# A Mamba scan on one Trainium2 core: last states through dA's first token, more C products on GpSimd, a later gate and a fourth C buffer

## The chip, the cores and the metric

The kernel runs on one core of one Trainium2 chip. The metric is the device time of one execution in microseconds (us). The core has five engines with a queue of instructions each: TensorE (PE in the profile), VectorE (DVE), ScalarE (ACT), GpSimd (POOL) and SyncE (SP), which issues nearly all DMAs here. An engine takes its instructions in order; one that waits holds back all behind it.

## What is computed

The reference runs two "metaformer" layers on x of shape (2, 96, 128, 128). Nearly all time goes to the mixer of layer 0, four Mamba scans (rows forward and backward, columns forward and backward) of 16,384 tokens, each with 192 channels and 16 states:

```python
def step(h, t):
    dt_t, u_t, B_t, C_t = t
    dA = jnp.exp(dt_t[:, :, None] * A)
    h = dA * h + dt_t[:, :, None] * B_t[:, None, :] * u_t[:, :, None]
    y = jnp.einsum('bds,bs->bd', h, C_t)
    return (h, y)
...
xz = x @ in_w.T                      # split into xc and z
xc = silu(conv4(xc) + conv_b)        # along the tokens
dt_raw, Bm, Cm = split(xc @ xproj_w.T)
dt = softplus(dt_raw @ dt_w.T + dt_b);  A = -exp(A_log)
y = (scan + Dp * xc) * silu(z);  out = y @ outp_w.T
```

The four results are joined, projected and added to x. Behind it come a quantized feed-forward layer, a 3x3 convolution and another feed-forward layer.

## The kernel before

For each of the two images the kernel normalizes x (`normalize`), runs the scans (`mamba`) and then the rest (`ffn_and_conv`). The change is in `mamba`.

**Tiles.** Two scans run together, a row scan and a column scan, so 2 x 192 channels fill three groups g of 128 partitions. The tokens go in blocks of T = 512. A *step* is one block of one pair: 32 blocks x 2 pairs = 64 steps an image, 128 in all. Within a step a *unit* is a group and two states; 3 x 8 = 24 units, numbered 0 to 23 (group 0 has 0 to 7, and so on). Unit k of the next step is written k'.

**The work of a unit.** ScalarE makes dA = exp(dt * A) for two states into a PSUM tile `da` (L349, three buffers, made two units ahead). A DMA broadcasts four states' B rows to 128 partitions (tile `row0`, 1 MB, for two units; L335), and GpSimd multiplies it by dt * u (`b_part`, L339). VectorE scans each state along the 512 tokens (`scan`, L353). The states are multiplied by the C rows (tile `row1`, again 1 MB for two units), on VectorE (L441) or, for units listed in `BY_POOL`, on GpSimd (`by_pool`, L360); for those the scan writes into the B tile instead of `da`. TensorE adds the products over the states with identity matmuls into the PSUM tile `y` (`sums`, L357; one buffer). After a group's eight units VectorE multiplies `y` by silu(z) (`gated`, the *gate*, L364), and TensorE starts the next group's `y` with the skip term (L448).

**State from step to step.** ScalarE copies each unit's last states to `hst` (L442). At the next step it makes `enter` = exp(dt of the first token * A) for a group (`entry`, L303); GpSimd multiplies that by `hst` (L342) and adds it to the first token of each B product (L343). The scan starts from 0.

**The order** is written out by hand in one loop over units; I call a turn of it *slot* k, and D(k) the time at which its first scan starts:

```python
if k % 2 == 0:
    fetch(k + 2 * B_AHEAD, 0, B_AHEAD, bs)   # B tile of units k+6, k+7
    feed(k + AHEAD)                          # GpSimd: B product of k+2, k+3
issue(k, 0)                                  # planned pieces
scan(0, da, b, hs[k])
behind(k - 1)     # C product, copy to hst, gate at a group's begin, sums
feed_decay(k + AHEAD)                        # ScalarE: dA of unit k+2
scan(1, da, b, hs[k])
if k % 2 == 0:
    fetch(k + 2 * C_AHEAD, 1, C_AHEAD, cs)   # C tile
issue(k, 1)                                  # planned pieces
```

`fetch` has as many buffers as it is ahead plus one, so each DMA, B or C, goes into the buffer that units k-2 and k-1 used. All stand in SyncE's one queue. F(k) is GpSimd's B product for units k and k+1, P(k) its C product of unit k, S(k) the sums of unit k; B(k) and C(k) are the DMAs of the tiles of units k and k+1. For a unit on GpSimd, P(k) is put in GpSimd's queue at the end of slot k+1, and S(k) in TensorE's at the end of slot k+3; for the others S(k) comes in slot k+1.

**Planned pieces** prepare the step after (`prologue`): at slot 21 the DMAs of its input, xa and xb (L228); at slots 1, 5 and 9 the input projection with the convolution folded in (*inx*, L211) of groups 1, 0, 2; at 7, 18 and 21 that of the z half (*inz*, L211, copied out at L247); silu of xc at slot 11 and of z at slot 7 (L259), softplus of dt at the end of slot 17 (L293), each between two table loads; the B, C and dt rows at slot 12; dt at 14 to 17 (L284, L289); dt * u (*dtu*, L298) at 19, and at 3 and 5 of the next step. At slots 19 and 3 of a step its outputs go through *project* (L372, L374) and are copied out. inx, inz, rows, dt and project share one PSUM tile, `misc`.

## Time and profile before

| | |
|---|---|
| median of 3 runs | 11,550.82 us (11,549.54 to 11,551.47) |
| the profiled execution, its own time | 11,556.77 us |
| its span | 11,555.0 us |
| PE, DVE, ACT, POOL busy over the span | 90%, 90%, 68%, 84% |
| one step in the middle of the second pair | 79.09 us |
| DMA | 3,417 MB, 87% of the 16 engines' time within a step |

The profile is one execution; times in it are us, or ns where marked. A line such as L357 is a line of the kernel. In a timeline the columns are start, length, engine, line, operation, output<-inputs, count, and in brackets the idle time ahead with what ended it. A matmul of 512 columns in f32 leaves two records, so a unit's sums are four. In a list of waits, the columns are the total, the number and the longest.

### The profile page before, as it was taken

To read this page: it belongs to the slowest core of one execution; us is meant where nothing else is said; L and a number is where in the kernel's file an instruction comes from. 1 tells how busy PE (TensorE), PEld (TensorE's weight loads), DVE (VectorE), ACT (ScalarE), POOL (GpSimd) and SP (SyncE) were. 2 spreads that over 40 slices of the span, in tenths; PEclk is the share of its full clock that TensorE was granted. 3 is DMA by queue.
4 is the path that set the end of the run, shared out by engine and by line. 5 is a ranking of instruction groups with operands and counts; after the bars stand their busy time and mean duration, and the time that the engine had idled before them with its cause. 6 is when DMAs were issued, how large, how long until landed. Compare 5 with 4: busy or idle time off the path is not lost. (4 is left out here: it accounts for less than half of the span.)

```text
span 11555.0 us, 94102 instructions
## 1 busy us (share of the span) xinstructions
PE 10435.0 (90%) x24208; PEld 3971.4 (34%) x24208; DVE 10421.6 (90%) x10127; ACT 7901.7 (68%) x13564; POOL 9672.3 (84%) x4700
## 2 busy tenths in 40 slices
PE   7999999999999999989989999999999999999899
PEld 2333333333333333333323333333333333333333
DVE  6999999999999999994469999999999999999944
ACT  6767767677677677665567677677676776776655
POOL 5999999999999999991159999999999999999911
PEclk8999999999999999999989999999999999999999
DMA  7888888888888888880068888888888888888800
GB/s 263 335 329 333 333 332 332 330 331 333 329 332 333 330 331 333 329 322 19 26 243 334 328 331 334 330 333 333 333 331 329 332 332 329 331 333 329 319 13 13
DMA packets 540755, 3416.96 MB, mean 296 GB/s; under 512 B 67532, under 2 KB 68652, under 8 KB 143832
## 3 DMA queue, kind: packets, MB, share of 16 engines
q1 hardware_dynamic: 539960, 3410.16, 76.8%
q8 instruction: 196, 3.21, 0.1%
q14 instruction: 343, 2.81, 0.1%
q0 software_dynamic: 256, 0.79, 0.0%
HBM read 3289.04 MB, written 54.53 MB: 289 GB/s over the span
## 5 line engine op out<-in xcount | busy, mean ns | idle before, releaser
L339 POOL TENSOR_TENSOR row<-dtu,row 128x2048 f32<-128x2048 f32 x1536 | 6948.9, 4524 | 283.3 <-DMA row<-bcd 281.6
L357 PE MATMUL y<-row,ident 128*128 128x512 f32 x12288 | 5690.6, 603 | 700.0 <-DVE row L441 699.9
L353 DVE TENSOR_TENSOR_SCAN da<-da,row 128x512 f32<-128x512 f32 x4608 | 5456.9, 1214 | 38.9 <-ACT da L349 5.2
L349 ACT ACTIVATE da<-dt,amat 128x512 f32<-128x512 f32 x6144 | 4246.9, 691 | 170.2
L357 PEld LDWEIGHTS y<-row,ident 128*128 128x128 f32 x12288 | 2256.8, 190 | 4008.4 <-issue 2243.5
L441 DVE TENSOR_TENSOR row<-da,row 128x1024 f32<-128x1024 f32 x2304 | 2776.7, 1205 | 70.2 <-DMA row<-bcd 70.0
L442 ACT COPY hst<-da 128x2 f32<-128x2 f32 x2304 | 368.9, 160 | 2652.2 <-DVE row L441 2649.3
L360 POOL TENSOR_TENSOR row<-row,row 128x1024 f32<-128x1024 f32 x768 | 1807.4, 2353 | 223.0 <-DVE row L353 147.5
L353 DVE TENSOR_TENSOR_SCAN row<-da,row 128x512 f32<-128x512 f32 x1536 | 1852.4, 1206 | 91.9 <-POOL row L339 84.1
L211 PE MATMUL misc<-xa,inx 96*64 96x512 f32 (+1 forms) x2048 | 946.1, 605 | 50.0 <-ACT mix L239 26.8
L211 PE MATMUL misc<-xb,inx 96*64 96x512 f32 (+1 forms) x2048 | 952.3, 608 | 33.6 <-ACT hst L442 24.2
L564 POOL TENSOR_TENSOR acc<-acc,y 96x512 f32<-96x512 f32 x128 | 147.4, 1151 | 991.5 <-DVE y L563 991.5
L298 POOL TENSOR_TENSOR dtu<-dt,xc 128x512 f32<-128x512 f32 x384 | 487.4, 1269 | 106.0 <-DMA xb<-xnc 99.8
L576 PE MATMUL pc<-pad,kw 96*96 96x512 f32 x1152 | 566.4, 593 | 0.0
L211 PEld LDWEIGHTS misc<-xa,inx 96*64 96x64 f32 (+1 forms) x2048 | 327.3, 165 | 581.2 <-issue 438.0
L448 PE MATMUL y<-xc,dmat 128*128 128x512 f32 x768 | 419.5, 628 | 103.6 <-DVE sz L364 103.6
L374 PE MATMUL misc<-sz,gmat 128*96 128x512 f32 x1024 | 484.1, 595 | 0.0
L284 PE MATMUL misc<-rows,dtw 12*128 12x512 f32 x768 | 434.3, 645 | 50.6 <-ACT dt L289 37.9
L364 DVE TENSOR_TENSOR sz<-y,sz 128x512 f32<-128x512 f32 x384 | 264.6, 689 | 229.5 <-PE y L357 198.0
L136 DVE TENSOR_TENSOR xq<-xm,rs 96x512 fp8e5<-96x512 f32 x128 | 87.9, 687 | 392.2 <-ACT rs L132 392.2
L211 PEld LDWEIGHTS misc<-xb,inx 96*64 96x64 f32 (+1 forms) x2048 | 316.5, 164 | 361.9 <-issue 214.1
L372 PE MATMUL misc<-acc,ident 96*96 96x512 f32 x512 | 387.6, 842 | 57.3 <-ACT sz L247 53.8
(76 smaller groups left out, 7449.9 us busy)
## 6 DMA issues: line engine op xcount, KB each, us to landing
row<-bcd SPq DMA_DIRECT2D x3072, 1024.0 KB, 7.4
xc<-mix SPq DMA_DIRECT2D x256, 128.0 KB, 5.4
sz<-mix SPq DMA_DIRECT2D x256, 128.0 KB, 8.9
xa<-xnr SPq DMA_DIRECT2D x124, 193.1 KB, 8.6
xb<-xnc SPq DMA_DIRECT2D x124, 193.1 KB, 8.7
bcd<-rows SPq DMA_DIRECT2D x128, 128.0 KB, 9.5
acc<-in_x_dram SPq DMA_DIRECT2D x16, 768.0 KB, 5.7
xnr<-xn SPq DMA_DIRECT2D x16, 768.0 KB, 4.3
```

Source lines behind the costliest of these rows:

```text
L211: nc.tensor.matmul(ps[rows, :], w(PAIRS[pi][d], k, lo, hi), src[d][:, k : k + T], **se)
L284: nc.tensor.matmul(d["ps"], w, d["rows"][0 : 2 * RK, :], start=True, stop=True)
L298: nc.gpsimd.tensor_tensor(dtu, d["dt"][:, g, :], d["xc"][:, g, :], ALU.mult)
L339: nc.gpsimd.tensor_tensor(b, d["dtu"][g][:, None, :].broadcast_to((128, 4, T)), b, ALU.mult)
L349: nc.scalar.activation(da[:, j, :], d["dt"][:, g, :], AF.Exp, scale=amat[:, pi, g, s + j : s + j + 1])
L353: nc.vector.tensor_tensor_scan(h[:, j, :], da[:, j, :], b[:, j, :], 0.0, ALU.mult, ALU.add)
L357: nc.tensor.matmul(y, ident, c[:, j, :], start=False, stop=s + j == S - 1)
L360: nc.gpsimd.tensor_tensor(c, h, c, ALU.mult)
L374: nc.tensor.matmul(d["po"], gmat[:, pi, 2 * g - 2 + k, :], d["yg"][g - 1 + k], start=False, stop=k == 1)
L441: nc.vector.tensor_tensor(c, h, c, ALU.mult)
L448: nc.tensor.matmul(y, dmat[:, pi, g, :], d["xc"][:, g, :], start=True, stop=False)
L576: nc.tensor.matmul(pc, kw[:, t, :], rows, start=t == 0, stop=t == 8)
```

## The change

The last states no longer enter through B. After the two exponentials of a unit, ScalarE multiplies the first token of each dA by the last state of that row of channels (a product on one column, in PSUM, with a pointer operand), and the scan starts from 1 instead of 0: the first step of the recursion then gives dA * h + B. `enter`, `entry` and GpSimd's products and adds on it are gone.

`BY_POOL` was units 0, 4, 8, 12, 16, 20; it is now 0, 3, 5, 8, 11, 13, 16, 19. As their sums come late, the last matmul of a group's `y` is that of unit 5, 13 and 23 (`LAST`). For a group's first unit `behind` now comes after the second scan of the slot, and with it the gate. The C tiles are fetched three pairs of units ahead, with four buffers, instead of two with three. The scratch for dynamic DMAs is set to 4,096.

```diff
-C_AHEAD = 2
+C_AHEAD = 3
-BY_POOL = tuple((g, s) for g in range(3) for s in (0, 8))
+BY_POOL = ((0, 0), (0, 6), (0, 10), (1, 0), (1, 6), (1, 10), (2, 0), (2, 6))
+LAST = [max(range(0, S, 2), key=lambda s: s + 5 * ((g, s) in BY_POOL)) for g in range(NG)]
...
-                def entry(g):
-                    nc.scalar.activation(enter[:, g, :], amat[:, pi, g, :], AF.Exp, scale=d["dt"][:, g, 0:1])
...
-            def b_part(i, d, g, s, b):
+            def b_part(d, g, b):
                 nc.gpsimd.tensor_tensor(b, d["dtu"][g][:, None, :].broadcast_to((128, 4, T)), b, ALU.mult)
-                if i > 0:
-                    if s == 0:
-                        nc.gpsimd.tensor_tensor(enter[:, g, :], enter[:, g, :], hst[:, g, :], ALU.mult)
-                    nc.gpsimd.tensor_tensor(b[:, :, 0], b[:, :, 0], enter[:, g, s : s + 4], ALU.add)
...
+                if i > 0:
+                    for j in range(2):
+                        nc.scalar.activation(da[:, j, 0:1], da[:, j, 0:1], AF.Copy, scale=hst[:, g, s + j : s + j + 1])
                 return da
...
-                nc.vector.tensor_tensor_scan(h[:, j, :], da[:, j, :], b[:, j, :], 0.0, ALU.mult, ALU.add)
+                nc.vector.tensor_tensor_scan(h[:, j, :], da[:, j, :], b[:, j, :], float(i > 0), ALU.mult, ALU.add)
...
-                    nc.tensor.matmul(y, ident, c[:, j, :], start=False, stop=s + j == S - 1)
+                    nc.tensor.matmul(y, ident, c[:, j, :], start=False, stop=(s, j) == (LAST[g], 1))
...
+            def gate_before(k):
+                pn, pu = divmod(k - 1, nu)
+                gated(steps[pn][0], state[pn], units[pu][0], ys.pop(k - 1))
+
+            def begins(k):
+                return 0 <= k < total and units[k % nu][1] == 0 and units[k % nu] in BY_POOL
...
-                if 0 < k <= total:
+                if 0 < k <= total and not begins(k - 1):
                     behind(k - 1)
                 feed_decay(k + AHEAD)
                 if k < total:
-                    scan(1, da, b, hs[k])
+                    scan(steps[n][1], 1, da, b, hs[k])
+                if begins(k - 1):
+                    behind(k - 1)
...
-    nc = bacc.Bacc("TRN2", target_bir_lowering=False, num_devices=1)
+    nc = bacc.Bacc("TRN2", target_bir_lowering=False, num_devices=1, dynamic_dma_scratch_size=4096)
```

More of the change, by code (lines that the diff above doesn't have):

```diff
@@ L194, in mamba @@
             hst = one.tile([128, NG, S], F32, name="hst")
-            enter = one.tile([128, NG, S], F32, name="enter")
             acc_w = acc.rearrange("c (h w) -> c w h", w=W)
@@ L321, in prologue @@
                     at += [(k, 0, partial(dt_u, g))]
-                    if i > 0:
-                        at += [((20, 24, 29)[g], 1, partial(entry, g))]
                 outs = (conv_out, gate_out, rows_out, dt_out)
@@ L336, in row_tile, with decay @@
                 return t
-            def b_part(i, d, g, s, b):
+            def b_part(d, g, b):
                 nc.gpsimd.tensor_tensor(b, d["dtu"][g][:, None, :].broadcast_to((128, 4, T)), b, ALU.mult)
-                if i > 0:
-                    if s == 0:
-                        nc.gpsimd.tensor_tensor(enter[:, g, :], enter[:, g, :], hst[:, g, :], ALU.mult)
-                    nc.gpsimd.tensor_tensor(b[:, :, 0], b[:, :, 0], enter[:, g, s : s + 4], ALU.add)
-            def decay(pi, d, g, s):
+            def decay(pi, i, d, g, s):
                 da = ps_w.tile([128, 2, T], F32, name="da")
@@ L349, in decay, with scan, sums @@
                     nc.scalar.activation(da[:, j, :], d["dt"][:, g, :], AF.Exp, scale=amat[:, pi, g, s + j : s + j + 1])
-                return da
-            def scan(j, da, b, h):
-                nc.vector.tensor_tensor_scan(h[:, j, :], da[:, j, :], b[:, j, :], 0.0, ALU.mult, ALU.add)
-            def sums(s, y, c):
+                if i > 0:
+                    for j in range(2):
+                        nc.scalar.activation(da[:, j, 0:1], da[:, j, 0:1], AF.Copy, scale=hst[:, g, s + j : s + j + 1])
+                return da
+            def scan(i, j, da, b, h):
+                nc.vector.tensor_tensor_scan(h[:, j, :], da[:, j, :], b[:, j, :], float(i > 0), ALU.mult, ALU.add)
+            def sums(g, s, y, c):
                 for j in range(2):
-                    nc.tensor.matmul(y, ident, c[:, j, :], start=False, stop=s + j == S - 1)
+                    nc.tensor.matmul(y, ident, c[:, j, :], start=False, stop=(s, j) == (LAST[g], 1))
             def by_pool(h, c):
@@ L425, in feed @@
                     n = k // nu
-                    b_part(steps[n][1], state[n], *units[k % nu], quads.pop(k))
+                    b_part(state[n], units[k % nu][0], quads.pop(k))
             def feed_decay(k):
@@ L430, in feed_decay @@
                     n = k // nu
-                    das[k] = decay(steps[n][0], state[n], *units[k % nu])
+                    das[k] = decay(*steps[n], state[n], *units[k % nu])
             ys = {}
+            def gate_before(k):
[3 more added lines that the diff above has]
+                return 0 <= k < total and units[k % nu][1] == 0 and units[k % nu] in BY_POOL
             def behind(k):
@@ L444, in behind @@
                     if k > 0:
-                        pn, pu = divmod(k - 1, nu)
-                        gated(steps[pn][0], state[pn], units[pu][0], ys.pop(k - 1))
+                        gate_before(k)
                     y = ps_y.tile([128, T], F32, name="y")
@@ L453, in behind @@
                     later(k + 1, 1, True, by_pool, h, c)
-                    later(k + 3, 1, True, sums, s, y, c)
+                    later(k + 3, 1, True, sums, g, s, y, c)
                 else:
-                    sums(s, y, c)
+                    sums(g, s, y, c)
                 if k == total - 1:
@@ L481, in mamba @@
                     hs[k] = b if (g, s) in BY_POOL else da
-                    scan(0, da, b, hs[k])
-                if 0 < k <= total:
+                    scan(steps[n][1], 0, da, b, hs[k])
+                if 0 < k <= total and not begins(k - 1):
                     behind(k - 1)
```

## The prediction

> **What bounds the kernel now.** I read the page's slices first (two stretches in which DVE, POOL and PE all show 9), then busy time over one step, then the waits of each engine, then the timelines of one step, engine by engine. Names are those of the section on the kernel: D(k) is when slot k begins, F, P and S are the B product, GpSimd's C product and the sums. The stage under change fills 128 steps of 79.09 us, 10,124 of 11,555 us. One step:

> ```profile
> core 0: us, PE busy (x) PEld busy (x) DVE busy (x) ACT busy (x) POOL busy (x), PEclk, DMA share, GB/s
> 8600.39:8679.48 79.09, 72.08 (x167) 28.16 (x167) 76.64 (x70) 55.85 (x97) 74.45 (x37) 1.00 0.87 332
> ```

> Four resources lie within 13% of each other, so no share of busy time prices this change; the order of the queues does. The waits (total us, times, longest):

> ```profile
> DVE sz L364 <- PE y L357: 198.0, 207, 3.1
> ...
> DVE row L441 <- DMA row<-bcd: 70.0, 121, 1.3
> ...
> POOL row L339 <- DMA row<-bcd: 281.6, 307, 3.6
> ...
> SPq L335 <- PE y L357: 6879.4, 1404, 11.1
> ```

> VectorE stalls little. But the DMA queue stands for 6,879 us behind C tiles whose buffer TensorE has not yet summed, and every later transfer stands behind them. ScalarE (first three lines) against VectorE (last two), around unit 13:

> ```profile
> 8641.74 1.28 ACT L260 ACT_TABLE_LOAD   x1
> 8643.03 0.16 ACT L442 COPY hst<-da 128x2 f32<-128x2 f32 x1
> 8643.23 1.42 ACT L349 ACTIVATE da<-dt,amat 128x512 f32<-128x512 f32 x2
> ```
> ```profile
> 8643.32 1.21 DVE L353 TENSOR_TENSOR_SCAN row<-da,row 128x512 f32<-128x512 f32 x1
> 8644.68 2.50 DVE L353 TENSOR_TENSOR_SCAN da<-da,row 128x512 f32<-128x512 f32 x2
> ```

> The scan starts 0.03 after the pair of exponentials ends (8643.23 + 1.42 = 8644.65), the same in the four steps behind it. After a silu (4.09 us with its two table loads) ScalarE is only just in time. At the end of the step, TensorE, then SyncE, then GpSimd:

> ```profile
> 8666.05 1.10 PE L372 MATMUL misc<-acc,ident 96*96 96x512 f32 x2 [0.42 <-ACT sz L247]
> 8666.99 1.88 PE L374 MATMUL misc<-sz,gmat 128*96 128x512 f32 x4
> 8668.71 5.31 PE L357 MATMUL y<-row,ident 128*128 128x512 f32 x12
> ```
> ```profile
> 8672.33 2.04 SPq L335 DMA_DIRECT2D row<-bcd  x3
> 8674.41 0.44 SPq L228 DMA_DIRECT2D xa<-xnr  x1
> 8674.89 0.44 SPq L228 DMA_DIRECT2D xb<-xnc  x1
> 8675.49 0.34 SPq L335 DMA_DIRECT2D row<-bcd  x1
> ```
> ```profile
> 8679.47 4.52 POOL L339 TENSOR_TENSOR row<-dtu,row 128x2048 f32<-128x2048 f32 x1 [0.62 <-DMA row<-bcd]
> 8684.07 0.20 POOL L343 TENSOR_TENSOR row<-row,enter 128x4 f32<-128x4 f32 x1
> 8684.23 2.36 POOL L360 TENSOR_TENSOR row<-row,row 128x1024 f32<-128x1024 f32 x1
> ```

> The twelve records are S(18), S(16), S(19). C(22) goes out as S(16) ends (8672.3), then B(2'), C(0') at 8674.05 as S(19) ends, xa, xb, B(4'). The four row tiles land 4.6, 6.7, 7.9 and 10.7 us after issue: 4.6 from a queue near empty, some 2.5 for each further one, 1.7 for xa and xb. F(2') starts when its tile lands; F(4') comes after P(0'), at 8686.55. Slot 0' begins at 8680.46, so B(4') goes out 5.0 us before it.

> **The change, by parts.** Pitches (start to start) from these timelines: scan and VectorE C product 1.12, gate 0.60, F 4.49, P 2.31, dtu 1.24, S 1.75 a unit, inx of group 1 3.6, of groups 0 and 2 3.44, project 3.49.

> *VectorE* loses two C products: 2.24 of 79.09 us. A slot is 3.36, or 2.24 where GpSimd has the product, 2.84 with a gate; 16, 5 and 3 of these make 73.5.

> *GpSimd* loses 12 adds (pitch 0.27 with the gap ahead, F to F 4.76) and 3 entry products (0.3), and gains two P: 12 x 4.49 + 8 x 2.31 + 3 x 1.24 = 76.1, against 12 x 4.76 + 6 x 2.31 + 3.7 + 0.9 = 75.6. No gain. Nor does VectorE hold GpSimd up: the six P of one step took 2.347 to 2.366, though scans and C products ran beside them.

> *ScalarE* loses three entry exponentials (0.29, hidden) and gains 48 products on one column. No row has it. Nearest: the copy of two columns out of PSUM, 0.160; a pointer operand adds 0.087 (L289 0.668 against L247 0.581); the upper end is the entry exponential, 0.294. I take 0.22 each, a little under 0.160 + 0.087 since it writes PSUM, and 0.04 of gap as between dependent instructions (L131 to L132): 0.52 a unit; 0.40 and 0.67 at the ends (0.160 and 0.294). Nothing less, since it only adds instructions. It is hidden in a plain slot, where ScalarE idles 1.1 to 1.8, but not behind a silu. [...]

> *Gate*: one scan later. Group 0's and 1's now wait for one more S (unit 5 or 13). It stood 1.55 us a step; I leave 0.5 to 0.8, inside the stretches below.

> *Fourth C buffer*: C goes out for two units further ahead, from the same slot and into the buffer of the same two units; the 0.55 us a step of L441 goes. It does not free the queue. Before, GpSimd's units are even: C of slot k waits for S(k-2), in TensorE's order one slot later. Now five of eight are odd: it waits for S(k-1), two slots later, after another unit's sums. Queued behind it on SyncE: the next B tile, at the step's end xa and xb too. That is the cost of this change. Odd units also free a B buffer later: before, P of a unit stood ahead of the next F in GpSimd's queue, now behind it; for unit 19 only F(0') lies between its P and F(2'), 4.49 against 5.2 from issue to start, which costs GpSimd 0.7 where it has slack. Smaller scratch: q0 carries 0.0%; nothing. The scan's initial 1.0: nothing.

> **Sum of a step.**
> Slots 10 to 13, ScalarE: before 10.33 (8634.35 to 8644.68), bound by pair, silu, pair; now two pairs are 0.52 longer, 11.35 (VectorE alone would need 8.96).
> Slots 13 to 16: 3.36 + 2.24 + 3.36 = 8.96.
> Slots 16 to 21: C product of unit 15 ends 2.33 after D(16); copy 0.23; pair 1.94; dt 0.6; pair 1.97; copy 0.1; softplus 4.09; copy 0.2; pair 1.94: D(20) at +13.5. Then sz 0.58, copy and pair: D(21) at +16.1. Before 17.5.
> Slots 21 to 24: three of 3.36, 10.1.
> Slots 0' to 10': project waits for that sz, D(16) + 14.0 (before + 12.2), which is 12.2 before D(0'). TensorE then runs through: project 3.49, S(18), S(16) 3.5, inz 0.97, S(20), S(21), S(19) 5.25: S(19) ends at D(0') + 1.05. C(2') waits for it, so it goes out at +1.1, then xa, xb, B(4') at +2.6; before, B(4') was out at -5.0. By the rows above C(2') lands at +5.7 and B(4') 4.2 later (10.7 - 7.9 + 1.4), +9.9. F(4') starts at +10.0 (before +6.1). From there GpSimd has no gap: F(4'), dtu, F(6'), P(3'), dtu, F(8'), P(5'), F(10') are 4 x 4.49 + 2 x 2.31 + 2 x 1.24 = 25.1. F(10') ends at +35.1, and slot 10' needs it. VectorE alone would be there at 30.3; it waits on the way, some 1.3 for F(4'), 2.5 for F(8'), 0.5 for F(10'). The other path is close: inx of group 1 needs xb (+7.4), and from there TensorE has 26.5 us without a gap up to the gate of slot 9' (inx 3.6, skip term 0.96, S of units 1, 2, 0, 4, 3, 6, 7, 5 at 14.0, project 3.49, inx of group 0 3.44, inz 1.0): gate at +33.9, D(10') at 34.5.
> Step: 35.1 + 11.35 + 8.96 + 16.1 + 10.1 = 81.6, that is 2.5 over 79.09. Some 126 steps see it (the ends of a batch do not): +315. The profiled execution took 11,556.8, 6 over the median, so 11,550.8 + 315 = 11,866.
> Bounds: six pairs lie in these stretches, so products at 0.40 to 0.67 move a step by -0.7 to +0.9; B(4') landing 1 us earlier moves it by -1.0: 79.9 to 82.5, or 11,653 to 11,980. That is the range of this case alone.

> **Rivals.**
> 1. The queue does not bite: TensorE is earlier at S(19), or the extra C lead gives SyncE room. Then slots 0 to 10 take 31.9 (ScalarE: D(7) 20.8 + 11.1 for pair, sz silu, pair), and the step is 31.9 + 46.5 = 78.4: -0.7 x 126, about 11,465. For it: only 2 us of GpSimd's idle time is DMA now. Against: five odd units.
> 2. The small products hide and GpSimd alone binds: 76.1, and 0.7 for B(2'), which is freed only one F (4.49) before it is needed and takes 5.2 to land: 76.8, about 11,262. Against: the three silus, already exact.
> 3. Slower without the queue: products at 0.67. Eight pairs behind the three silus give 78.4 + 8 x 0.15 = 79.6, about 11,615. ScalarE decides from 0.6 a unit up.
> 4. What is saved and added cancels, within 0.2% (about what a measurement here can tell from none): 0.18 us a step.

> **Chances.** The queue 0.70, rival 1 0.13, 2 0.07, 3 0.05, 4 0.05: faster 0.20, same 0.05, slower 0.75. The range takes in the first case, 3, 4 and about rival 1: 11,450 to 11,980.

> **What would show it.** Right: B(4') issued after slot 0' has begun; SyncE's wait on L357 still thousands of us; VectorE waiting for L339 (84 us before) for some 500 us, at slots 4 and 8; GpSimd idle before L339 for DMA well over 282 us; inx waiting for xb; the L441 wait near nothing; the new products near 0.22. Wrong: L339 waits under 100 us, or the stretch from slot 10 to 13 not longer than 10.3.

## The result, and the profile after

The changed kernel takes 11,953.99 us (median of 4 runs, 11,935.16 to 11,974.88) against 11,550.18 for the kernel before on the same chip: a ratio of 1.035, 95% interval 1.0331 to 1.037. The profiled execution took 11,964.59 us, its span 11,962.8; its granted TensorE clock over the span was 0.970, before 0.989. It is slower, by 88 us more than predicted (11,866).

From the page of the changed kernel: the engines' busy time, then groups (busy total, mean ns, idle ahead and what ended it).

```profile
PE 10636.5 (89%) x24208; PEld 4112.9 (34%) x24208; DVE 10226.2 (85%) x9871; ACT 8916.3 (75%) x19144; POOL 9901.9 (83%) x3096
...
L331 POOL TENSOR_TENSOR row<-dtu,row 128x2048 f32<-128x2048 f32 x1536 | 6941.4, 4522 | 803.7 <-DMA row<-bcd 676.0
...
L211 PE MATMUL misc<-xa,inx 96*64 96x512 f32 (+1 forms) x2048 | 1084.5, 679 | 329.4 <-DMA xa<-xnr 264.6
L340 ACT ACTIVATE da<-da,hst 128x1 f32<-128x1 f32 x5952 | 1149.8, 232 | 96.3
```

VectorE is busy 85% instead of 90%, and nothing came of it. The new products (L340) take 0.232 each. GpSimd's B product (L331, before L339) now idles 676 us for its tile where it idled 282, and the input projection (L211) waits 265 us for xa. The waits of the changed kernel (total us, times, longest), then those of SyncE's queue:

```profile
DVE row L344 <- POOL row L331: 337.4, 130, 43.1
...
DVE sz L355 <- PE y L348: 251.7, 256, 3.4
...
DVE row L344 <- ACT da L340: 216.5, 122, 1.8
...
DVE da L344 <- POOL row L331: 173.0, 163, 3.2
```
```profile
SPq L327 <- PE y L348: 6364.4, 1403, 16.1
```

VectorE waits 510 us for the B product (337.4 + 173.0; 84 before) and 217 for the decay with its new products. SyncE's wait for the sums is about as large as before in total, but its longest is 16.1 instead of 11.1. One step of the changed kernel at the places shown of before, first ScalarE and VectorE around unit 13:

```profile
8621.02 1.28 ACT L260 ACT_TABLE_LOAD   x1
8622.32 0.16 ACT L440 COPY hst<-da 128x2 f32<-128x2 f32 x1
8622.37 1.42 ACT L337 ACTIVATE da<-dt,amat 128x512 f32<-128x512 f32 x2
8623.83 0.39 ACT L340 ACTIVATE da<-da,hst 128x1 f32<-128x1 f32 x2
```
```profile
8624.25 1.22 DVE L344 TENSOR_TENSOR_SCAN row<-da,row 128x512 f32<-128x512 f32 x1 [1.75 <-ACT da L340]
```

The scan of unit 13 now starts 0.03 after the two products end (8623.83 + 0.39 = 8624.22): they stand on the path, 0.42 a unit with the gap ahead of them. SyncE, then GpSimd, at the step's end; slot 0' begins at 8659.74:

```profile
8657.46 0.32 SPq L327 DMA_DIRECT2D row<-bcd  x1
8657.83 0.42 SPq L226 DMA_DIRECT2D xa<-xnr  x1
8658.30 0.43 SPq L226 DMA_DIRECT2D xb<-xnc  x1
8658.83 2.08 SPq L327 DMA_DIRECT2D row<-bcd  x3
```
```profile
8668.26 4.54 POOL L331 TENSOR_TENSOR row<-dtu,row 128x2048 f32<-128x2048 f32 x1 [1.16 <-DMA row<-bcd]
```

C(2'), held by the late sums, goes out at 8657.46, then xa, xb, and at 8658.83 B(4'): 0.9 before slot 0' instead of 5.0 before it. Over the steps of the second image the median is 0.90 (from 1.0 before slot 0' to 1.0 after it), and 4.95 in the kernel before. F(4') starts at 8668.26, 8.5 into the step (before 6.1).

That is the part predicted. The other shows in the windows of single steps (each from one silu of z to the next; the columns are the length, the busy time of five engines with counts, the granted clock, the DMA share and GB/s):

```profile
core 0: us, PE busy (x) PEld busy (x) DVE busy (x) ACT busy (x) POOL busy (x), PEclk, DMA share, GB/s
...
8608.10:8688.60 80.50, 72.64 (x168) 27.73 (x167) 73.92 (x67) 64.33 (x142) 75.62 (x25) 1.00 0.87 328
8688.60:8774.08 85.48, 75.55 (x166) 29.40 (x165) 77.02 (x70) 59.94 (x121) 76.75 (x24) 0.94 0.81 305
...
9349.92:9436.16 86.24, 76.25 (x167) 30.08 (x166) 77.95 (x70) 63.78 (x141) 76.75 (x24) 0.94 0.79 303
```

Steps of the same work last 80.5 at full clock and 86.2 at 0.94. The second row, 85.5 at 0.94, leads into the first step of the second pair of scans, whose units have no products, so that ScalarE has some 20 instructions fewer in it; it is long all the same. There TensorE stands still for 4.26 us ahead of inx, waiting for xa, and runs on at half speed (TensorE's timeline; a record of inx takes 1.06 to 1.11 instead of 0.59), with the clock by stretches below it:

```profile
8749.15 1.08 PE L211 MATMUL misc<-xa,inx 96*64 96x512 f32 x1 [4.26 <-DMA xa<-xnr]
8749.81 1.11 PE L211 MATMUL misc<-xb,inx 96*64 96x512 f32 x1
```
```profile
8747.00:8751.00 4.00, 1.85 (x5) 1.02 (x7) 2.46 (x3) 0.08 (x1) 3.81 (x2) 0.63 0.99 308
8751.00:8755.00 4.00, 4.00 (x12) 1.75 (x10) 4.00 (x4) 1.46 (x3) 2.72 (x1) 0.51 1.02 422
8755.00:8759.00 4.00, 4.00 (x12) 1.47 (x9) 2.50 (x3) 2.93 (x7) 4.00 (x3) 1.00 1.02 424
```

Such windows over all steps between 6,300 and 11,300 us (55 to 60 in each kernel) give the table that the rest is read from. "At full clock" are the steps whose clock reads 1.00. Each ratio is against runs of the kernel before on the same chip.

| kernel | time, us | ratio (95%) | mean step | at full clock (steps) | mean clock |
|---|---|---|---|---|---|
| before | 11,550.18 | 1 | 79.23 | 79.23 (56 of 57) | 0.999 |
| after | 11,953.99 | 1.035 (1.0331 to 1.037) | 82.63 | 80.84 (22 of 60) | 0.976 |
| a1_c_lead_2 | 11,513.9 | 0.9972 (0.9962 to 0.9982) | 78.92 | 78.90 (33 of 57) | 0.991 |
| a2_early_x | 11,886.45 | 1.0299 (1.0281 to 1.0316) | 81.84 | 80.78 (23 of 59) | 0.979 |
| a3_no_product | 11,468.52 | 0.9934 (0.9919 to 0.9949) | 78.68 | 78.30 (48 of 56) | 0.997 |
| a4_even_six | 12,196.11 | 1.0566 (1.055 to 1.0582) | 84.28 | 79.47 (1 of 58) | 0.949 |
| b1_product_only | 11,945.31 | 1.0352 (1.0334 to 1.0369) | 82.26 | 81.24 (31 of 60) | 0.985 |
| b2_c_slack_before | 11,537.63 | 0.9993 (0.9984 to 1.0003) | 79.09 | 79.09 (56 of 57) | 1.00 |
| b3_filler | 11,929.52 | 1.0331 (1.0316 to 1.0347) | 82.20 | 81.92 (42 of 60) | 0.993 |
| b4_project_later | 11,609.12 | 1.0055 (1.004 to 1.007) | 79.67 | 79.67 (58 of 58) | 1.00 |
| b5_c_ahead_only | 11,951.51 | 1.0354 (1.034 to 1.0369) | 82.37 | none of 60 | 0.971 |
| c1_product_slack | 12,108.74 | 1.0491 (1.0475 to 1.0508) | 83.86 | 80.40 (4 of 58) | 0.958 |
| c2_no_product_slack | 11,312.4 | 0.9799 (0.9785 to 0.9812) | 77.29 | 77.29 (54 of 55) | 0.999 |
| c3_one_project_later | 11,514.05 | 0.9973 (0.9963 to 0.9983) | 78.92 | 78.92 (56 of 57) | 0.999 |

One of these steps in each kernel is the first of the second pair of scans, which has some 30 of ScalarE's instructions less. It is a4's only step at full clock, and one of c1's four; the other three take 80.69.

So the 3.4 us that a step grew by are 1.6 at full clock (80.84 - 79.23), the kind of loss that was predicted, and 1.8 (82.63 - 80.84) from the steps where the clock fell, which was not. Not all of the 1.8 is slower matmuls: over all steps TensorE is busy 73.83 us and idle 8.81, in those at full clock 72.46 and 8.38, so that 1.4 of it is longer matmuls and 0.4 more idle time. Times 126 that is 428, where the two profiled executions differ by 408; the steps in the table are those of the second image alone, and the 20 us between were not followed further.

### The profile page after: what moved, and what is told of

It reads as the page before. It is cut to its first block, busy times and chain, and to the rows that moved or that the text cites. A ratio compares the mean times of both kernels' runs of the same rounds, so it can differ in the third digit from the quotient of the medians.

```text
span 11962.8 us, 98334 instructions
## 1 busy us (share of the span) xinstructions
PE 10636.5 (89%) x24208; PEld 4112.9 (34%) x24208; DVE 10226.2 (85%) x9871; ACT 8916.3 (75%) x19144; POOL 9901.9 (83%) x3096
## 4 chain that ended last, share of the span: by engine, by line
PE 30%; ACT 22%; DVE 19%; DMA 10%; POOL 9%; issue 9%; SPq 1%; POOLq 0%; DVEq 0%; ACTq 0%
PE y L348 10%; ACT da L337 9%; DVE da L344 8%; POOL row L331 7%; DMA row<-bcd 5%; PE misc L211 5%; DVE row L439 5%; DVE row L344 4%; PE pc L575 4%; DMA xa<-xnr 4%; PE misc L365 3%; ACT da L340 2%; PE xm L123 2%; PE v L129 2%; PE misc L363 2%
## 5 line engine op out<-in xcount | busy, mean ns | idle before, releaser
L331 POOL TENSOR_TENSOR row<-dtu,row 128x2048 f32<-128x2048 f32 x1536 | 6941.4, 4522 | 803.7 <-DMA row<-bcd 676.0
L344 DVE TENSOR_TENSOR_SCAN da<-da,row 128x512 f32<-128x512 f32 x4096 | 4932.2, 1218 | 215.2 <-POOL row L331 173.0
L344 DVE TENSOR_TENSOR_SCAN row<-da,row 128x512 f32<-128x512 f32 x2048 | 2471.9, 1207 | 562.7 <-POOL row L331 337.4
L439 DVE TENSOR_TENSOR row<-da,row 128x1024 f32<-128x1024 f32 x2048 | 2460.4, 1201 | 0.1
L351 POOL TENSOR_TENSOR row<-row,row 128x1024 f32<-128x1024 f32 x1024 | 2411.4, 2355 | 0.0
L440 ACT COPY hst<-da 128x2 f32<-128x2 f32 x2048 | 332.9, 163 | 1420.7 <-DVE row L439 1416.8
L211 PE MATMUL misc<-xa,inx 96*64 96x512 f32 (+1 forms) x2048 | 1084.5, 679 | 329.4 <-DMA xa<-xnr 264.6
L340 ACT ACTIVATE da<-da,hst 128x1 f32<-128x1 f32 x5952 | 1149.8, 232 | 96.3
L211 PE MATMUL misc<-xb,inx 96*64 96x512 f32 (+1 forms) x2048 | 1074.0, 673 | 6.1 <-DMA xb<-xnc 4.6
L211 PEld LDWEIGHTS misc<-xa,inx 96*64 96x64 f32 (+1 forms) x2048 | 356.7, 180 | 792.3 <-issue 533.1
L365 PE MATMUL misc<-sz,gmat 128*96 128x512 f32 x1024 | 544.6, 658 | 0.0
L211 PEld LDWEIGHTS misc<-xb,inx 96*64 96x64 f32 (+1 forms) x2048 | 356.4, 180 | 439.3 <-issue 358.8
L284 PE MATMUL misc<-rows,dtw 12*128 12x512 f32 x768 | 434.2, 645 | 78.9 <-ACT rows L272 72.5
L355 DVE TENSOR_TENSOR sz<-y,sz 128x512 f32<-128x512 f32 x384 | 263.1, 685 | 252.7 <-PE y L348 251.7
## 6 DMA issues: line engine op xcount, KB each, us to landing
sz<-mix SPq DMA_DIRECT2D x256, 128.0 KB, 10.3
```

The costliest lines, as they stand in the source:

```text
L211: nc.tensor.matmul(ps[rows, :], w(PAIRS[pi][d], k, lo, hi), src[d][:, k : k + T], **se)
L331: nc.gpsimd.tensor_tensor(b, d["dtu"][g][:, None, :].broadcast_to((128, 4, T)), b, ALU.mult)
L340: nc.scalar.activation(da[:, j, 0:1], da[:, j, 0:1], AF.Copy, scale=hst[:, g, s + j : s + j + 1])
L344: nc.vector.tensor_tensor_scan(h[:, j, :], da[:, j, :], b[:, j, :], float(i > 0), ALU.mult, ALU.add)
L351: nc.gpsimd.tensor_tensor(c, h, c, ALU.mult)
L365: nc.tensor.matmul(d["po"], gmat[:, pi, 2 * g - 2 + k, :], d["yg"][g - 1 + k], start=False, stop=k == 1)
```

## The experiments

Three theories. *Queue*: the late sums of the odd units hold a C tile, and xa, xb and B(4') stand behind it on SyncE. *ScalarE*: the small products alone make the loss. *Clock*: TensorE's short waits drop its granted clock, and the lost clock costs time. All kernels named a, and b3, b4, c2, c3, start from the changed kernel; b1, b2, b5 and c1 from the one before.

### Freeing the queue: a1_c_lead_2

Four C buffers, but the tile is fetched only two pairs ahead, so that it finds a buffer freed one pair earlier.

```diff
+C_LEAD = 2
-            for m, (n, ahead) in ((bs, (0, B_AHEAD)), (cs, (1, C_AHEAD))):
-                for k in range(ahead):
+            for m, (n, ahead, lead) in ((bs, (0, B_AHEAD, B_AHEAD)), (cs, (1, C_AHEAD, C_LEAD))):
+                for k in range(lead):
-                    fetch(k + 2 * C_AHEAD, 1, C_AHEAD, cs)
+                    fetch(k + 2 * C_LEAD, 1, C_AHEAD, cs)
```

> The changed kernel, but with four C buffers each C tile is fetched only two pairs of units ahead, as before the change: the DMA then goes into the buffer of units k-4 and k-3 instead of k-2 and k-1. Queue theory (late sums of odd units hold the C tile, and xa, xb and the B tile behind it): B(4') goes out some 4 us before slot 0' instead of 1 to 3 us after it, inx no longer waits for xa (265 us before), VectorE's wait for L331 falls from 510 to under 150 us, a step takes about 78.5, all in all 11,450 to 11,560. ScalarE theory (the 48 small products make the loss): the queue is only a symptom, steps stay at 80.4 or more, over 11,720.

Measured: 11,513.9 us, 440 less than the changed kernel, and below the one before. In its waits TensorE's sums hold SyncE 996 us (6,364 in the changed kernel); it now waits for ScalarE's copies (3,074.5) and GpSimd's C products (2,367.0) instead, with room to spare, since GpSimd's wait for B tiles is nearly gone (64 us; 676):

```profile
DVE row L345 <- POOL row L332: 88.0, 8, 42.5
...
POOL row L332 <- DMA row<-bcd: 63.8, 96, 3.8
```
```profile
SPq L328 <- PE y L349: 996.4, 558, 3.4
```

B(4') goes out 5.00 us before slot 0' (median), as it did before the change, instead of 0.90. The queue theory stands so far: with sums and products in the same order as in the changed kernel, moving the fetch by one pair takes the whole loss away. Of the 3.7 us a step that this brings, 1.9 is seen at full clock (80.84 - 78.90); the rest goes with the clock. Its steps are 78.95 whether the clock dips or not:

```profile
8125.67:8204.62 78.95, 72.99 (x168) 27.80 (x166) 74.71 (x68) 64.20 (x142) 76.11 (x24) 0.98 0.85 333
8204.62:8283.57 78.95, 71.56 (x168) 27.16 (x166) 74.71 (x68) 64.34 (x142) 76.12 (x24) 1.00 0.85 332
```

### The products: a3_no_product and c2_no_product_slack

a3 takes ScalarE's products out of the changed kernel and scans from 0; c2 does the same with the fetch of a1.

```diff
-                if i > 0:
-                    for j in range(2):
-                        nc.scalar.activation(da[:, j, 0:1], da[:, j, 0:1], AF.Copy, scale=hst[:, g, s + j : s + j + 1])
-                ... float(i > 0), ALU.mult, ALU.add)
+                ... 0.0, ALU.mult, ALU.add)
```

> The changed kernel without ScalarE's 48 products a step, the scan starting from 0: last states do not enter the next block, so this part of the computation is left out. Queue theory: slots 10 to 13 fall from 11.05 to about 10.2 and slots 16 to 21 from 16.1 to about 14.8, slots 0 to 10 stay near 34 as B(4') is still late; VectorE still waits some 500 us for L331; steps of 78.4 and some longer ones from the clock, 11,560 to 11,720. ScalarE theory: all of the loss goes and more, steps near 77, under 11,400.

> Kernel a3 (the changed kernel without ScalarE's products, so that last states do not enter, which is left out) with the C tiles fetched two pairs ahead into four buffers. It shows what the change would bring with neither cost. Theory: GpSimd binds (12 B products, 8 C products, 3 dtu: 76.1 us a step): steps of 76.3 to 77.3, 11,200 to 11,340. Rival (a3 is bound elsewhere, TensorE's stretch from slot 0 to 9 or the silus): 77.4 and more, 11,400 to 11,470 as a3.

Measured: 11,468.52 and 11,312.4. a3 lies between the two numbers on record: each theory holds half of it. In a3 B(4') is as late as in the changed kernel (0.97 us before slot 0'), but VectorE waits only 276 us for the B product (510 with the products; some 500 was expected). With a1 they make a square, in mean steps:

| | queue held | queue free |
|---|---|---|
| with products | 82.63 (after) | 78.92 (a1) |
| without | 78.68 (a3) | 77.29 (c2) |

Neither part alone makes the loss. Products cost 1.6 a step where the queue is free and 4.0 where it is held; the queue costs 1.4 without them and 3.7 with them. At full clock the held queue costs 1.9 with products (80.84 - 78.90) and 1.0 without (78.30 - 77.29). In c2 GpSimd is nearly always busy, 76.1 of 77.28, so it is close to what bounds.

```profile
8132.81:8210.09 77.28, 71.83 (x168) 27.08 (x166) 74.71 (x68) 55.14 (x93) 76.12 (x26) 1.00 0.87 339
```

### The products alone, on the kernel before: b1_product_only

```diff
+                if i > 0:
+                    for j in range(2):
+                        nc.scalar.activation(da[:, j, 0:1], da[:, j, 0:1], AF.Copy, scale=hst[:, g, s + j : s + j + 1])
-            def scan(j, da, b, h):
+            def scan(i, j, da, b, h):
...
-                if i > 0:
-                    if s == 0:
-                        nc.gpsimd.tensor_tensor(enter[:, g, :], enter[:, g, :], hst[:, g, :], ALU.mult)
-                    nc.gpsimd.tensor_tensor(b[:, :, 0], b[:, :, 0], enter[:, g, s : s + 4], ALU.add)
```

> The kernel before with one part of the change: the last states enter through ScalarE's 48 products a step and a scan that starts from 1; GpSimd's units, the gate and the C buffers as before. Theory: the products cost by themselves, at the three silus (0.42 measured for a pair) some 1.5 us a step: 80 to 81, 11,660 to 11,800. If the lower granted clock comes from waits of TensorE for ScalarE (rows, project) as in a4, some steps are longer still: 11,800 to 12,200, clock under 0.975. Rival: the products hide and GpSimd, freed of 3.9 us of adds, makes it faster: under 11,530.

Measured: 11,945.31, the whole loss of the change without its GpSimd units, its gate or its fourth buffer. At full clock a step is 81.24, 2.0 over before, though GpSimd's adds are gone; on top of it come the steps with the clock down. The waits for the gate doubled (408.5 us; 198 before). So the products are dearer on the old schedule than on the new one with a free queue (1.6); why, no run takes apart.

### The queue on the kernel before: b2_c_slack_before and b5_c_ahead_only

b2 gives the kernel before a1's four buffers with the old lead; b5 only `C_AHEAD = 3` and the smaller scratch, as in the change.

```diff
-C_AHEAD = 2
+C_AHEAD = 3
+C_LEAD = 2          # b2 only, used as in a1
...
+ ... dynamic_dma_scratch_size=4096)
```

> The kernel before with one part: a fourth C buffer, used as slack (still fetched two pairs of units ahead, into the buffer of units k-4 and k-3), and the smaller scratch. Queue theory: SyncE's wait for L357 (6,879 us) falls under 2,000 us and VectorE's waits for the C tile (70 us) go; but TensorE's stretch from slot 0 to 9 and ScalarE's silus stay, so a step of 78.3 to 79.0, 11,440 to 11,540. Rival (the queue binds nothing before): 11,550 as it is.

> The kernel before with the change's C_AHEAD = 3 (four buffers, three pairs of units ahead) and the smaller scratch alone. Queue theory: the C tiles still go into the buffers of units k-2 and k-1, so SyncE waits for L357 as long as before, and only VectorE's 70 us for C tiles go: 11,490 to 11,560. Rival (a fourth buffer frees the queue however it is used): SyncE's wait for L357 halves.

Measured: b2 11,537.63, no difference; SyncE's wait for the sums fell from 6,879 to 2,300 us (it waits 4,985 for VectorE's scans instead), and B(4') went out 6.50 us before slot 0' instead of 4.95, so those thousands of us bounded nothing before. b5: 11,951.51, 3.5% slower from one more buffer, where I expected next to nothing. SyncE waits 7,131 us, as before, B(4') goes out 5.00 us before slot 0', as before, and the waits of VectorE for C are gone, as expected. So one buffer more does not hold the queue by itself: in the changed kernel it takes the new list of GpSimd's units with it, as a3 shows. But no step of b5 ran at full clock. The line through its sixty steps (80.0 + 82 x (1 - clock)) would put it 0.8 over before's 79.2 without that, an estimate, since no step lies there. TensorE's timeline in one step, and the clock there:

```profile
8209.17 1.12 PE L284 MATMUL misc<-rows,dtw 12*128 12x512 f32 x2 [1.27 <-ACT rows L272]
8210.60 3.12 PE L357 MATMUL y<-row,ident 128*128 128x512 f32 x4 [0.31 <-DVE row L441]
```
```profile
8206.00:8210.00 4.00, 2.73 (x7) 0.86 (x5) 3.97 (x4) 3.06 (x6) 4.00 (x2) 1.00 1.01 410
8210.00:8212.00 2.00, 1.69 (x4) 0.68 (x4) 2.00 (x3) 1.35 (x3) 1.95 (x2) 0.83 0.99 397
8212.00:8214.00 2.00, 2.00 (x4) 0.50 (x3) 2.00 (x3) 0.85 (x3) 1.97 (x2) 0.50 1.00 369
...
8220.00:8222.00 2.00, 2.00 (x4) 0.67 (x2) 0.00 (x0) 0.00 (x0) 2.00 (x2) 0.61 0.00 0
```

TensorE idles 1.27 us for ScalarE's copy of the rows and 0.31 for VectorE, and then has half a clock for 10.2 us (in most steps 3.4), in which four records take 3.12 instead of 1.88 and VectorE runs dry (0.00 busy at 8,220). Why one more buffer opens just this gap (S comes earlier, ScalarE's copy does not) is argued from the two timelines, not shown by a run.

### Products with a free queue, on the kernel before: c1_product_slack

b1 with a1's fetch.

```diff
-C_AHEAD = 2
+C_AHEAD = 3
+C_LEAD = 2
```

> Kernel b1 (the kernel before, with last states through ScalarE's products) plus a fourth C buffer used as slack, two pairs of units ahead. Theory: the products' price reaches the step through the DMA queue; they delay project and the sums behind it on TensorE, C tiles wait for those sums, B tiles behind them. With the queue freed only what VectorE waits for at the silus is left: steps of 79.3 to 80.3, no more 86, 11,580 to 11,710. Rival (the products cost what they cost on the path from dA to the scan, queue or not): 11,880 or more, as b1.

Measured: 12,108.74, slower than b1; the number on record for a free queue fell. The queue is free, B(4') goes out 5.94 us before slot 0' (4.04 in b1), and at full clock a step takes 80.69, 0.55 less than in b1; the clock takes more than that. It is the cleanest picture of the clock. Three steps of it:

```profile
7639.40:7720.09 80.69, 71.82 (x167) 27.17 (x167) 76.41 (x70) 64.36 (x141) 71.55 (x22) 1.00 0.86 328
...
8294.46:8376.51 82.05, 73.41 (x167) 27.68 (x167) 76.41 (x70) 64.44 (x142) 71.60 (x22) 0.98 0.85 324
8376.51:8461.85 85.34, 76.70 (x167) 28.59 (x166) 76.40 (x70) 64.39 (x141) 71.51 (x22) 0.94 0.81 309
```

The same 167 matmul records take 71.82, 73.41 and 76.70 us; from the first to the last they take 4.88 more, and the step is 4.65 longer. Here nearly every us that the clock takes from TensorE is a us of time. The drop follows an idle time of 1.60 us ahead of the dt matmul:

```profile
8484.16 1.52 PE L285 MATMUL misc<-rows,dtw 12*128 12x512 f32 x2 [1.60 <-ACT rows L273]
```

But the same 1.60 us stands there in the step at full clock. In all fourteen kernels each stretch at half clock is a whole number of pieces of 3.41 us, which lie on one fixed grid through the whole run: of 405 stretches between 6,300 us and the last step, 280 are one piece long, 60 two, 59 three and 6 four. Here are pieces of that grid in c1, around the gap in the step at full clock and, below the dots, around the one above:

```profile
7658.74:7662.15 3.41, 1.81 (x5) 0.59 (x4) 3.38 (x4) 2.81 (x9) 3.41 (x2) 1.00 0.62 252
7662.15:7665.56 3.41, 3.18 (x8) 0.97 (x6) 3.41 (x5) 2.53 (x6) 3.41 (x2) 1.00 0.99 375
...
8481.35:8484.76 3.41, 1.81 (x5) 0.48 (x3) 3.41 (x4) 2.69 (x9) 3.41 (x2) 1.00 0.67 221
8484.76:8488.17 3.41, 3.41 (x5) 1.18 (x4) 3.41 (x4) 2.58 (x7) 3.41 (x2) 0.50 1.00 363
```

In c1 a piece with this gap whole inside it keeps TensorE busy for 1.81 us, 53%. Of the 58 pieces at full clock that were busy between 50 and 55%, 55 were followed by half clock, and the one in the step at full clock is among the three that were not; of the 1,278 that were busier, none was.

### The late sums: a4_even_six

The changed kernel with the old list of GpSimd's units.

```diff
-BY_POOL = ((0, 0), (0, 6), (0, 10), (1, 0), (1, 6), (1, 10), (2, 0), (2, 6))
+BY_POOL = tuple((g, s) for g in range(3) for s in (0, 8))
```

> The changed kernel with GpSimd's units as before the change: 0, 4, 8, 12, 16, 20. Queue theory: sums are late by one slot again, xa is there in time and VectorE's wait for L331 falls under 150 us; VectorE has two C products more (2.24 us a step) and ScalarE its products, so a step of 79.5 to 80.5, 11,600 to 11,740. ScalarE theory: slower than the changed kernel's 80.6 in the undisturbed steps, since VectorE has more to do and ScalarE as much: 81.5 or more, over 11,860.

Measured: 12,196.11, the slowest of all; my number for the queue theory (below 11,740) fell. The old list frees part of the queue: B(4') goes out 2.53 us before slot 0' (0.90 in the changed kernel, 5.00 in a1), while GpSimd still waits 774 us for its tiles. What made it slower than the changed kernel is the clock, as far as the steps tell: it was 1.00 in only one step of 58, and 0.949 in the mean. TensorE stands 2.52 us ahead of the dt matmul in the step shown:

```profile
8030.04 2.07 PE L284 MATMUL misc<-rows,dtw 12*128 12x512 f32 x2 [2.52 <-ACT rows L272]
```

and is granted 0.50 from 8,030 to 8,042. The run does not price the late sums, since it changes the clock far more than the queue.

### The clock in the changed kernel: a2_early_x and b3_filler

a2 loads xa and xb two slots earlier; b3 puts four useless matmuls into TensorE's queue ahead of inx.

```diff
-                at = [(-3, 1, load), ...
+                at = [(-5, 1, load), ...                      # a2, prepared 3 slots earlier
+                at = [(1, 0, filler), (-3, 1, load), ...      # b3
+                    for _ in range(4):
+                        nc.tensor.matmul(ps, ident, dmat.rearrange("p a b c -> p (a b c)")[:, 0:T], start=True, stop=True)
```

> The changed kernel, with the DMAs of xa and xb put into SyncE's queue at the end of slot 19 instead of slot 21, so ahead of the B and C tiles of unit 2'. Clock theory (steps over 81.5 are those in which TensorE idles for xa and then runs at a lower granted clock): the wait for xa goes, the granted clock goes back to 0.98 to 0.99, the steps are all near 80.6, for B(4') is still late: 11,700 to 11,780. Its rival (the lower clock is from the mix of work, whatever inx waits for): clock 0.97 and 11,900 or more.

> The changed kernel with four useless matmuls (128x128 on 512 columns, 3.5 us) put ahead of the first input projection, into its PSUM tile, so that TensorE is busy while it waits for xa. Clock theory: it no longer idles long enough there, the granted clock rises to 0.98 or more, the steps over 84 us go, and with 3.5 us more work the kernel is not slower: 11,750 to 11,950. Rival (the clock has another cause, or the wait itself is the price): 3.5 us more on the path to the gate, 12,050 to 12,400, clock 0.97.

Measured: a2 11,886.45, between its two numbers. The wait for xa is gone, and the steps over 84 with it, but the clock is no better (0.979 against 0.976 over the steps): it now falls after the 1.99 us that TensorE stands ahead of project (0.54 from 8,105 to 8,108 in one step). b3 11,929.52, within what the clock theory gave. The mean clock rose from 0.976 to 0.993, and no step is over 84.7 (87.1 in the changed kernel), but a step at full clock is 81.9 instead of 80.8, since the filler takes TensorE's time. So the work that filled the gap raised the clock, and cost nearly all that it brought: 24 us are left (11,953.99 to 11,929.52).

### Closing project's gap: b4_project_later and c3_one_project_later

a1 still idles 1.99 us ahead of project, and in some steps its clock is 0.50 for 3.4 us behind it. Both kernels are a1 with project at the end of its slot instead of its beginning, b4 in slots 19 and 3, c3 in slot 19 alone.

```diff
-                    later(k + 4, 0, True, project, pi, i, d, g)
+                    later(k + 4, 1, True, project, pi, i, d, g)              # b4
+                    later(k + 4, int(g == 1), True, project, pi, i, d, g)    # c3
```

> The kernel a1 (four C buffers, fetched two pairs ahead) with project put at the end of its slot, behind the sums of the unit before, instead of ahead of them. TensorE idles 2.0 us before project in each step of a1, for the copy of z out of their common tile, and the granted clock falls to 0.59 right after. Clock theory: the idle time goes, clock 0.99, steps from 78.95 to 78.0 to 78.7, 11,390 to 11,490. Rival (ScalarE's products bind the step by the scans behind the silus alone): 11,500 to 11,530 as a1.

> Kernel a1 with project of slot 19 alone put behind the sums of its slot; project of slot 3 stays ahead of the sums, where it fills TensorE's time before the C product of unit 2 (b4 moved both and lost that: 1.4 us of idle time ahead of three sums). Clock theory: no idle time of 2 us ahead of project, clock 0.99, steps from 78.95 to 78.2 to 78.9, 11,420 to 11,510. Rival (TensorE has time enough there; the step is set between slots 0 and 13): 11,505 to 11,520, as a1.

Measured: b4 11,609.12, slower than a1 by 95 though its stage ran at full clock: project of slot 3 had filled TensorE's time ahead of S(2), and without it the gate of slot 9 waits 2.16. c3 11,514.05, the same as a1, with the clock at 1.00 instead of 0.99 over the stage. The drop in a1 was off the path: there the lost clock cost no time (its steps shown take 78.95 at 0.98 and at 1.00). The version that beats both kernels, by 0.3%, is a1 (or c3, the same within the intervals).

## Why the prediction was right, and where its sum was not

**The mechanism** held but for one link. C(2') waits for sums; xa, xb and B(4') go out behind it; F(4') starts late; VectorE starves. a1 shows it: let C(2') go earlier and 440 us are gone. The link is which sums. In each of 60 steps C(2') left when eight records behind inz had ended, two units' sums and in the code's order S(20) and S(21); S(19), the late sum of the odd unit, had only begun. And in the step shown B(2') went out at 8653.59, before P(19) ended at 8654.36. So neither waited for what the prediction, and the rule of units k-2 and k-1 in the section on the kernel before, says; which buffers they got the profile does not show. Every sign named was there but three: in most steps B(4') was issued just before slot 0' and not after it, inx waited for xa and not xb, and VectorE's wait in the step shown is 2.16 at slot 8 with none at slot 4.

**The step's sum**, 81.6, against the undisturbed step of the profile (clock 1.00): slots 10 to 13 11.05 (predicted 11.35), 13 to 16 9.13 (8.96), 16 to 21 16.13 (16.1), 21 to 24 10.23 (10.1), 0' to 10' 34.08 (35.1), together 80.6.

- *10 to 13* failed by 0.3 through the price of the products: 0.42 a unit, not 0.52. One is 0.232 (0.22 taken), but a pair lasts 0.39, since the two overlap (end to end they would take 0.464). The 0.027 that I took off the copy and the pointer (0.160 + 0.087) for the write to PSUM is about what the rows of before give at 512 columns: L349, from SBUF into PSUM with a pointer, takes 0.691, and L132, within SBUF, without one and on 96 partitions, 0.630, with 0.087 for the pointer 0.717.
- *0' to 10'* failed in the term "TensorE then runs through": from project's start to C(2') I took 13.25 us, and it was 10.6 (8646.89 to 8657.46). Project took 2.65 before the next sums, not 3.49, as the prediction's own lines had it (8666.05 to 8668.71): 3.49 is near the project of slot 3, 3.43 in the step shown (8672.38 to 8675.81). inz had ended 6.9 after project's start where I had 8.0; and C(2') was let go 3.6 after inz, the length of two units' sums and not three. Together with a project that began 0.65 earlier against slot 0' this put B(4') 3.5 earlier than predicted, F(4') 1.5 earlier, and the stretch 1.0 shorter.
- *The gate* moved the other way: I left 0.5 to 0.8 a step of its wait, and it waited 251.7 us in all (198 before), 2.0 a step.

**The step that failed outright** is one that isn't in the sum. It took each TensorE duration from a profile in which the clock read 1.00, and held it fixed while it added idle time to TensorE. In the changed kernel the clock fell behind some of those idle times, and the steps in which it fell cost 1.8 us a step in the mean, 1.4 of it in longer matmuls. That is a little more than the rest of the change together, 1.6 at full clock; and the 1.6 is itself a balance, since without queue and products (c2) a step takes 77.3, so that these two cost 3.55 and the rest brings 1.94. The two errors, -0.9 a step on the predicted mechanism (80.84 against 81.6, and 79.23 against 79.09) and +1.8 for the missing one, are why the total came out near: that it is only 88 us off is luck. By full clock alone I would estimate 1.6 x 126, some 200 us of loss, slower all the same.

**The rivals.** "The queue does not bite" was priced at 78.4 a step; a1, where it does not, has 78.9. "GpSimd alone binds", at 76.8, needs the products gone too: c2 has 77.3, with GpSimd busy 76.1 as worked out. "Slower without the queue" was priced at 79.6 with the dearest products; on the old schedule c1, with a free queue and products of 0.42, takes 80.7 at full clock, so the price of extra work behind the silus was too low there. The changed kernel needs both the queue and the products to be slower than the one before: a1 and a3, with one of them each, are faster than it.

How much of the 1.8 belongs to which gap stays open. No run closed all of TensorE's gaps in the changed kernel and left its queue as it was; a2 and b3 each close one, and the clock then falls behind another.

## What to carry to other kernels

Ask first what each transfer waits for: the prefetch further ahead did not free SyncE's queue, whose C tiles still waited for the sums (6,364 us; 6,879 before), and in the changed kernel the same four buffers with a shorter lead did (a1, 996). Look at what stands behind the waiting transfer, not at the total of the wait: of the 6,879 us in the kernel before two thirds could go without a gain (b2), while in the changed one, with 6,364, the shorter lead brought 440. And on TensorE, 89% busy in the changed kernel, an added idle time was not only its own length: half clock followed on 228 of the 281 pieces of 3.41 us in which it was busy for less than half, and in c1 4.88 us more of the same matmuls made a step 4.65 longer. So price the work behind such a gap at the lower clock too, and look at the granted clock of single steps before believing any sum.
